# K projection by quarters, the residual added in DRAM, the first convolutions together at the end, and rotary tables scaled in place: one change to an attention and convolution kernel

## The chip, the cores and the metric

The kernel runs on one core of one Trainium2 chip. The metric is the device time of one execution in microseconds (us). All data are fp32. Engines are called by their profile names: PE (TensorE, matrix multiplication; PEld is its weight load), DVE (VectorE), ACT (ScalarE), POOL (GpSimd) and SP (SyncE, which here only issues DMAs). DMAs with addition on the way (accumulates) are issued by POOL, plain loads and stores mostly by SP.

## The reference

Two layers on x of shape (4, 1024, 32, 32): 4 batches, 1024 channels, 1024 tokens (pixels). The first is attention with rotary angles, an RMS norm of q and of k over all channels, 16 heads of 64, a projection, an RMS norm and a residual:

```python
x = hidden_states.reshape(B, C, N).transpose(0, 2, 1)
residual = x
qkv = (x @ w_qkv.T + b_qkv).reshape(B, N, 3, nh, hd)
q, k, v = (qkv[:, :, 0], qkv[:, :, 1], qkv[:, :, 2])
q = _apply_rope(q, cos, sin)
k = _apply_rope(k, cos, sin)
q = _rmsnorm(q.reshape(B, N, inner), q_norm_w).reshape(B, N, nh, hd)
k = _rmsnorm(k.reshape(B, N, inner), k_norm_w).reshape(B, N, nh, hd)
scores = jnp.einsum('bqhd,bkhd->bhqk', q, k) * scale
attn = jax.nn.softmax(scores, axis=-1)
ctx = jnp.einsum('bhqk,bkhd->bqhd', attn, v).reshape(B, N, inner)
out = ctx @ w_proj.T
out = _rmsnorm(out, norm_out_w)
out = out + residual
```

The second is a bottleneck block. Its norms are over all batches, so no later convolution can start before the first one has seen all four:

```python
out = jax.nn.relu(_bn(_conv(x, w1, b1, 1, 0), g1, be1))    # 1x1, 1024 -> 256
out = jax.nn.relu(_bn(_conv(out, w2, b2, 1, 1), g2, be2))  # 3x3, 256 -> 256
out = _bn(_conv(out, w3, b3, 1, 0), g3, be3)               # 1x1, 256 -> 1024
out = jax.nn.softplus(residual_scale)[0] * out
out = x + out
return jax.nn.relu(out)
```

## The kernel before

**Stages.** For each batch b: the projections q, k and v, attention, and the projection y of its result. Channels lie on the 128 partitions in 8 blocks, tokens along the free axis, so q(b), k(b) and y(b) are 8 blocks of 128 x 1024. After the four batches come the first convolutions conv1 of batches 1, 2 and 3, then the 3x3 convolution (with Winograd's transform) and the last 1x1 convolution. conv1(0) alone stands earlier, between q(1) and k(1) (L937 to L941). x1 = layer 0's result goes through DRAM in x1d: o_norm writes it (L805), read_back (L899) fetches it for conv1, and the end reads it again (L1194).

**Projections.** They use Strassen's scheme in Winograd's form. `project` (L283) is one level: 7 products of 512 x 512 x 512 blocks in place of 8, each in 4 groups of 4 matmuls of 128x512, 112 in all. `project2` (L415), "by quarters", applies the scheme again within each of the 7: 49 products, each 4 matmuls of 128x256, 196 in all. It costs more sums: DVE makes four inner sums of operands for each k (L446), adds products that can't be summed in PSUM (L466, L468), and makes block sums of 128x1024 (L487); ACT copies products out of PSUM (L501 to L544). Its weights come as 7 loads of 256 KB for each of the 7 outer products (L421): three straight from the weights or the one-level sums, four from wd2 in DRAM, which `prepare` (L393) has written before (4 loads, 4 DVE sums, 4 stores of 256 KB). One load is issued by SP as one of the wring's 8 slots comes free. q, v and y of b = 1 to 3 go by quarters; k of every batch, and all of b = 0, go by one level. wd2 has three planes: WQ, WV, WP. WQ's seven and three of WV's are prepared in attention of b = 0, the other four of WV in y(0), WP's in attention of b = 1.

**Rotary angles and norm.** `qk_proj` (L552) sums the squares over the channels beside the projection; the q, k bias goes into the Square pass (L560) and, for q, into the rotation. `inverse_rms` (L651) makes the sums over partitions on PE (ss_q, ss_k, ss_y), a reciprocal on DVE, and spreads it over all partitions through DRAM (inv_d, L670 and L671). `rope` (L676) multiplies cos and sin tables by it (L680 to L682; cosT x norm goes to a buffer of its own, rc, sinT x norm into total), and then rotates the 8 blocks one by one ("turn": two DVE operations of 128x1024, then two accumulating DMAs of 256 KB on POOL, L694).

**Attention** (L728). 16 steps (8 pairs of heads for each half of the tokens), each 14.6 us of PE: scores, Exp on ACT, the denominators' sums on DVE, and the product with v. The list `extra` (L773) puts one step of other work, such as a `prepare`, behind each.

**Residual.** o_norm (L798) runs beside the next batch's q stage: for each block DVE scales y (L803), POOL accumulates x from DRAM onto y in SBUF (y<-in_x_dram, L804, 512 KB), and when this has landed it writes y to x1d (x1df<-y, L805, 512 KB). The last batch uses last_norm, with DVE adding x.

**What sets the order.** PE's order is that of the source. The order on the other engines is made by a scheduler, so that a line may be issued earlier than where it stands. Within the source, a small pacing machine places the side work: `after(n, step)` (L243) runs a step n products later, `waiting` is a queue of (cost, step) of which `product_done` (L246) takes as many as DVE has room for, and `rest` (L262) drains both, for instance at the end of v (L947).

**Buffers.** y(b) and k(b) share one buffer (pool kp), so k(b+1) can be written only when y(b) has been stored. x(b+1), attention's probabilities and x1 read back share another (xp). The 16 "units" of scratch for q by quarters lie in a room that later holds v.

Of the kernel before, what the change touches and what calls it, by code (L numbers as in the profile page):

```python
# [11 lines left out]
F32 = mybir.dt.float32  # L12
AF = mybir.ActivationFunctionType
# [72 lines left out]
def program(ctx, tc, x, wblk, w2, w3, vecs, cos, sin, out, bad):  # L86
# [24 lines left out]
    def col(name, i=0):  # L111
        return vec[:, COL[name] + i : COL[name] + i + 1]
# [31 lines left out]

    wd = dram.tile([4 * NG, len(SUMS), P, NH * P], F32, name=f"wd{u}")

    wd2 = dram.tile([3, len(OUTER), len(SUMS), P, CH], F32, name=f"wd2{u}")
    dens = dram.tile([P, CH], F32, name=f"dens{u}")
    inv_d = dram.tile([3 * B, N], F32, name=f"inv_d{u}")
    norms_done = list(range(3 * B))  # L150
# [2 lines left out]
    with tc.tile_pool(name=f"st{u}", bufs=2) as st, ExitStack() as s:  # L153
# [10 lines left out]

        cosT = tp.tile([P, N], F32, tag="cos", name="cosT")
        sinT = tp.tile([P, N], F32, tag="sin", name="sinT")
        ident = None
        if bad is None:
            ident = kv.tile([P, P], F32, name="ident")
# [38 lines left out]
        def flat(t):  # L208
            return t.rearrange("p a b -> p (a b)")
# [37 lines left out]
        def after(n, step):  # L247
            later.append((pace["at"] + n, step))
# [13 lines left out]
            spend(cost)  # L262
            step()

        def rest():
            while later or waiting:
                product_done()

        def sums(ts, bs, i):
# [279 lines left out]
                    product_done(H2)  # L549
            pace["hold"] = False  # L550

        def qk_proj(b, base, bs, ts, bias, dst, tag, w1=None, two=None):  # L552

            total = acc.tile([P, N], F32, tag="tot", name=f"sq{tag}_{b}")
            seen = set()

            def outs(g):
                return [dst[:, f, h] for f in (g, g + NG) for h in half]

            def squares(at, c, bias=None):  # L560
                bias = 0.0 if bias is None else bias
                if c not in seen:
                    seen.add(c)
                    nc.scalar.activation(total[:, half[c]], at, AF.Square, bias=bias)
                    return
                sq = temp(f"sq_{tag}_{b}")
                nc.scalar.activation(sq, at, AF.Square, bias=bias)  # L567

                def more():
                    spend(TT)  # L570
                    nc.vector.tensor_tensor(total[:, half[c]], total[:, half[c]], sq, ALU.add)  # L571

                after(0.5, more)

            if two is None:
                project(b, base, bs, ts, outs, bias, squares, False, tag, w1)
                return total

            def ready(c):
                ob, tb = (int(i) - 1 for i in c)  # L580
                for i in range(NG):
                    f = ob * NG + i
                    after(
                        0.5 * (i // 2 + 1),
                        lambda f=f: squares(dst[:, f, half[tb]], tb, col(bias, f) if bias else None),
                    )

            project2(b, two[0], base, two[1], two[2], two[3], dst, False, tag, ready)
            return total
# [83 lines left out]

            after(4, root)

        def rope(b, dst, total, eps, scale, w, tag, rc, biased=True):  # L676

            def tables():  # L680
                nc.vector.tensor_tensor(rc, cosT, total, ALU.mult)
                nc.vector.tensor_tensor(total, sinT, total, ALU.mult)  # L682

            def turn(f):
                k, other = dst[:, f, :], big_temp(f"{tag}s_{b}_{f}")
                for i, (t, table) in enumerate(((other, total), (k, rc))):
                    if w is not None:
                        nc.vector.scalar_tensor_tensor(t, k, w[i][:, f : f + 1], table, ALU.mult, ALU.mult)  # L688
                    elif biased:
                        nc.vector.tensor_tensor(t, k, table, ALU.mult)  # L690
                    else:
                        nc.vector.scalar_tensor_tensor(t, k, col("bq", f), table, ALU.add, ALU.mult)
                for i in range(2):
                    nc.gpsimd.dma_start(dst[i::2, f, :], other[1 - i :: 2, :], accum_op=ALU.add)  # L694

            def then():
                waiting.append((4 * TT, tables))
                for f in range(NT):
                    waiting.append((4 * TT, lambda f=f: turn(f)))

            inverse_rms(total, eps, scale, f"{tag}_{b}", then)
# [26 lines left out]
        def attention(b, c, q_all, k_all, v, probs_, late, ready, extra):  # L728
# [4 lines left out]
            for hp in range(NHP):  # L733
# [35 lines left out]
                if hp % 2 == 1:  # L769
                    for r in ready:  # L770
                        mean_of_v(q_all, *r)
                    ready.clear()
                if extra:  # L773
                    extra.pop(0)()
                if hp % 2 == 0:
                    continue
# [21 lines left out]
        def o_norm(b, total, ys):  # L798


            def norm(f):
                y = ys[:, f, :]
                nc.vector.scalar_tensor_tensor(y, y, col("ow", f), total, ALU.mult, ALU.mult)  # L803
                nc.gpsimd.dma_start(y, x[b, f * P : (f + 1) * P, :], accum_op=ALU.add)  # L804
                nc.gpsimd.dma_start(x1d[f, :, b * N : (b + 1) * N], y)  # L805
# [20 lines left out]
        def conv1_weights(name):  # L826
            return [[block(W1, f, ih, f"c1_{name}_{f}_{ih}") for ih in range(2)] for f in range(NPT)]
# [75 lines left out]
        def x_tile(b):  # L903
            return xp.tile([P, NT, N], F32, tag="x", name=f"x_{b}")
# [19 lines left out]
        nc.sync.dma_start(cosT, cos)  # L924
        for i in range(2):

            nc.sync.dma_start(sinT[i::2, :], sin[1 - i :: 2, :])
        queue_sums(ts[0], xs[0])
        room = v_room("rq_0")
        for b in range(B):  # L930
# [4 lines left out]
            tq = qk_proj(b, WQ, xs[b], ts[b], "bq", q_all, "q", w1 if b == 0 else None, two)  # L935
            rope(b, q_all, tq, eps_q, HD / C, None, "q", flat(room[:, 2:3, :]), b == 0)
# [48 lines left out]
            if b + 1 < B:  # L985
                xs[b + 1] = x_tile(b + 1)
                ts[b + 1] = t_tiles(b + 1)
                rows = (0, 1, 4, 5, 2, 3, 6, 7)
                for j in range(NT):

                    def load(b=b, i=rows[j]):
                        for c in range(NCH):
                            load_x(b + 1, c, (i,))

                    after(3 + 1.5 * j, load)
                for i in range(0, NH, 2):

                    def queue(b=b, i=i):
                        waiting.append((7 * TT, lambda: sums(ts[b + 1], xs[b + 1], i)))

                    after(3 + 1.5 * (2 * i + 3) + 2, queue)
                if b == 0:
                    for k in range(3, len(OUTER)):
                        after(5 * (k - 3) + 0.5, lambda k=k: after(4, prepare(1, WV, k, big_pieces)))
            else:
                back = {B - 3: x_tile(b + 1)}
                for i in range(NT):
                    after(8 + 1.5 * i, lambda i=i: read_back(B - 3, (i,)))
            yt[b] = kp.tile([P, NT, N], F32, tag="k", name=f"y_{b}")
            two = (2, *in_place(q_all, tc_, yt[b], False)) if b > 0 else None  # L1010
            ty = qk_proj(b, WP, q_all, tc_, None, yt[b], "y", None, two)
# [3 lines left out]
                xr = v_room("xr")  # L1015
                last_norm(b, ty, yt[b], xr)

        back[B - 2] = kv.tile([P, NT, N], F32, tag="q", name="back")
        read_back(B - 2)
# [342 lines left out]
```

## Time and profile before

| what | value |
|---|---|
| time, median of 3 runs | 2771.21 us (2770.35 to 2775.1) |
| the profiled execution | 2769.1 us |
| its span | 2767.3 us |
| mean granted PE clock | 0.995 |
| DMA moved in the span | 390.27 MB, mean 141 GB/s |

Some of its groups of instructions (line, engine, operation, out<-in, shapes and count; then busy us, mean ns of one; then idle time before them and what ended it):

```profile
L756 DVE TENSOR_TENSOR den<-den,p 128x1024 f32<-128x1024 f32 x384 | 470.5, 1225 | 41.4 <-ACT p L752 0.9
L571 DVE TENSOR_TENSOR sqk<-sqk,sq_k 128x512 f32<-128x512 f32 x56 | 37.9, 688 | 56.1 <-ACT sq_k L567 54.8
L316 ACT COPY k<-pa_k 128x512 f32<-128x512 f32 x48 | 28.1, 586 | 116.3 <-PE pa_k L297 116.3
```

A DVE operation on 128x512 takes 0.688 us, on 128x1024 about 1.22. Each fp32 matmul shows as two PE records, and PEld's weight loads overlap them. Three more stages, in the columns of a table by stage (window, length, busy us of each engine with its count, mean granted clock, DMA share, GB/s):

```profile
361.00:448.00 87.00, 87.00 (x408) 31.70 (x408) 82.25 (x76) 47.86 (x54) 25.40 (x31) 1.00 0.52 164
536.16:632.49 96.33, 96.33 (x226) 42.76 (x226) 59.98 (x74) 18.58 (x32) 22.75 (x35) 1.00 0.72 243
2443.10:2526.40 83.30, 83.30 (x203) 36.66 (x202) 45.26 (x70) 14.12 (x21) 3.23 (x4) 1.00 0.65 232
```

They are three pairs of attention steps of b = 0 with their preparations, y(0), and conv1 of batches 1, 2 and 3.

### The profile page before, as it was taken

What the parts mean: (1) busy time and instruction counts of PE and PEld (TensorE: products, weight loads), DVE (VectorE), ACT (ScalarE), POOL (GpSimd) and SP (SyncE); (2) the same over time, 40 slices, a digit from 0 to 9 for tenths busy, and PEclk for the clock granted to TensorE, in tenths of its full rate; (3) what the DMA queues carried; (4) which work ended last, traced back from release to release, by engine and by line L of the source; (5) the groups of instructions that cost most, each with busy time, mean ns of one, the idle gap of its engine ahead of it and who ended that gap; (6) DMA issues with size and microseconds to landing.
All of it is one profiled execution on the core that took longest, in us unless ns stands there. A gap on an engine that the chain in (4) does not pass through costs nothing.

```text
span 2767.3 us, 31322 instructions
## 1 busy us (share of the span) xinstructions
PE 2727.7 (99%) x11242; PEld 1561.1 (56%) x11242; DVE 1955.9 (71%) x2213; ACT 1029.5 (37%) x1407; POOL 368.9 (13%) x419
## 2 busy tenths in 40 slices
PE   9999999999999999999999999999999999999997
PEld 4449533347647633488648433688467333856853
DVE  4355599765645898787648777887648977767987
ACT  1221455422222455423222555332223555222266
POOL 1033022121010121101011100101201110100000
PEclk9999999999999999999999999999999999999999
DMA  5366254276555552167567210459647010672165
GB/s 206 107 171 174 82 168 139 73 268 195 177 137 152 149 156 79 41 206 210 177 143 196 53 24 16 149 151 264 148 131 201 16 24 16 202 270 84 62 216 211
DMA packets 213157, 390.27 MB, mean 141 GB/s; under 512 B 24768, under 2 KB 97008, under 8 KB 212992
## 3 DMA queue, kind: packets, MB, share of 16 engines
q1 hardware_dynamic: 181856, 284.24, 32.7%
q0 software_dynamic: 31136, 103.92, 15.0%
q8 instruction: 92, 1.51, 0.2%
q14 instruction: 73, 0.60, 0.1%
HBM read 260.88 MB, written 76.86 MB: 122 GB/s over the span
## 4 chain that ended last, share of the span: by engine, by line
PE 97%; DMA 2%; DVE 1%; ACT 0%; issue 0%; SPq 0%; ACTq 0%
PE sc L745 16%; PE cx L762 16%; PE p_v L436 9%; PE p_y L441 9%; PE p_q L441 9%; PE pa_k L297 8%; PE c L833 4%; PE pc_k L297 4%; PE c L1266 4%; PE pa_q L297 2%; PE pa_v L305 2%; PE pb_k L297 2%; PE pa_y L297 2%; PE c2x L1127 2%; PE c2y L1127 2%; DMA w_q<-wdf 1%
## 5 line engine op out<-in xcount | busy, mean ns | idle before, releaser
L756 DVE TENSOR_TENSOR den<-den,p 128x1024 f32<-128x1024 f32 x384 | 470.5, 1225 | 41.4 <-ACT p L752 0.9
L752 ACT ACTIVATE p<-sc 128x1024 f32<-128x1024 f32 x512 | 476.2, 1043 | 55.0 <-PE sc L745 53.5
L745 PE MATMUL sc<-q,k 64*128 64x512 f32 x2048 | 457.2, 596 | 2.2 <-DVE v L468 1.6
L762 PE MATMUL cx<-p,v 128*64 128x512 f32 x2048 | 453.6, 595 | 0.0
L745 PEld LDWEIGHTS sc<-q,k 64*128 64x128 f32 x2048 | 190.9, 186 | 266.3 <-issue 121.4
L762 PEld LDWEIGHTS cx<-p,v 128*64 128x64 f32 x2048 | 141.4, 137 | 304.3 <-issue 304.3
L726 POOL TENSOR_SCALAR q<-q,vec 128x512 f32<-128x512 f32 x64 | 125.9, 1973 | 665.8 <-DVE q L725 665.8
L767 ACT COPY q<-cx 128x512 f32<-128x512 f32 x64 | 37.5, 586 | 357.2 <-PE cx L762 357.2
L441 PE MATMUL p_y<-q,w_y 128*128 128x256 f32 x696 | 157.5, 380 | 0.0
L436 PE MATMUL p_v<-w_v,x 128*128 128x256 f32 x696 | 157.1, 379 | 0.0
L441 PE MATMUL p_q<-to,w_q 128*128 128x256 f32 x672 | 154.5, 384 | 0.0
L754 DVE TENSOR_TENSOR den<-p 128x1024 f32<-128x1024 f32 x64 | 76.5, 1196 | 99.8 <-ACT p L752 99.8
L441 PEld LDWEIGHTS p_y<-q,w_y 128*128 128x128 f32 x696 | 131.8, 190 | 20.7 <-issue 2.5
L436 PEld LDWEIGHTS p_v<-w_v,x 128*128 128x128 f32 x696 | 132.2, 190 | 19.3 <-issue 1.4
L441 PEld LDWEIGHTS p_q<-to,w_q 128*128 128x128 f32 x672 | 129.2, 193 | 19.6 <-issue 1.6
L787 DVE RECIPROCAL rec<-dn 128x512 f32<-128x512 f32 x32 | 107.3, 3353 | 28.8 <-PE dn L781 28.7
L1266 PE MATMUL c<-h,w 128*128 128x512 f32 x256 | 110.3, 592 | 0.9 <-ACT h L1170 0.9
L1266 PEld LDWEIGHTS c<-h,w 128*128 128x128 f32 x256 | 48.6, 190 | 62.1 <-issue 54.3
L694 POOL DMA_DIRECT2D k<-ks x64 | 55.3, 1010 | 205.0 <-DVE k L688 123.9
L571 DVE TENSOR_TENSOR sqk<-sqk,sq_k 128x512 f32<-128x512 f32 x56 | 37.9, 688 | 56.1 <-ACT sq_k L567 54.8
L316 ACT COPY k<-pa_k 128x512 f32<-128x512 f32 x48 | 28.1, 586 | 116.3 <-PE pa_k L297 116.3
L571 DVE TENSOR_TENSOR sqq<-sqq,sq_q 128x512 f32<-128x512 f32 x56 | 38.4, 690 | 44.5 <-ACT sq_q L567 42.0
(535 smaller groups left out, 4116.8 us busy)
## 6 DMA issues: line engine op xcount, KB each, us to landing
w_q<-wd2f SPq DMA_DIRECT2D x84, 256.0 KB
w_v<-wd2f SPq DMA_DIRECT2D x84, 256.0 KB
w_y<-wd2f SPq DMA_DIRECT2D x84, 256.0 KB
wd2f<-w_pre POOLq DMA_DIRECT2D x68, 256.0 KB, 2.7
x<-in_x_dram SPq DMA_DIRECT2D x64, 256.0 KB
q<-qs POOLq DMA_DIRECT2D x64, 256.0 KB, 5.1
k<-ks POOLq DMA_DIRECT2D x64, 256.0 KB, 5.2
inv<-rec SPq DMA_DIRECT2D x256, 64.0 KB
```

Of the source, the lines that this page charges most:

```text
L297: nc.tensor.matmul(o, w[:, i, :], r(i), start=first and i == 0, stop=last and i == NH - 1, skip_group_check=True,)
L436: nc.tensor.matmul(o[:, q].rearrange("p (g f) -> p g f", g=2), r[:, i, q * P : (q + 1) * P], wt[:, :, i, :], skip_group_check=True, **at,)
L441: nc.tensor.matmul(o[:, q], wt[:, q, i, :], r[:, i, :], skip_group_check=True, **at)
L726: nc.gpsimd.tensor_scalar(cx, cx, col("bv", hp), None, ALU.add)
L745: nc.tensor.matmul(sc[:, j], k_all[d, hp, t * P : (t + 1) * P], q_all[d, hp, at], start=True, stop=bad is not None,)
L752: nc.scalar.activation(p, sc, AF.Exp)
L756: nc.vector.tensor_tensor(d_, d_, p, ALU.add)
L762: nc.tensor.matmul(o[j * HD : (j + 1) * HD, :], v[:, t, h0 : h0 + HD], probs[t][:, j], start=(t == 0), stop=(t == N // P - 1),)
L787: nc.vector.reciprocal(r, dn)
L833: nc.tensor.matmul(o, w[f][ih][:, ii, :], ys[:, i, half[c]], start=(i == 0), stop=(i == NT - 1))
L1127: nc.tensor.matmul(o[:, r * TR * TC : (r + 1) * TR * TC], uw[2 * h + r, j][:, i * PL + f * P : i * PL + (f + 1) * P], vt[b, i][:, 2 * h + ...
L1266: nc.tensor.matmul(os[i], w3t[k][f // NH][:, f % NH, :], h2[b, k][:, half[c]], start=(k == 0), stop=(k == NPT - 1),)
```

## The change

- k of b = 1 to 3 goes by quarters. wd2 gets a fourth plane for WK. WV's seven are all prepared in attention of b = 0, with WK's first; WK's other six in y(0). In k the bias is added by an ACT pass of its own, in place, before the square; q keeps the old way (`bias_later`).
- o_norm no longer adds x: it writes y to x1d. In the source of the next batch, before its attention, stand 8 accumulates from x in DRAM onto x1d in DRAM.
- conv1(0) leaves its place between q(1) and k(1) and comes after conv1(2) at the end; its x1 is read back into xp's buffer.
- cosT and sinT are multiplied by the norm in place; rc is gone. After the last turn of every rope but the last, both are loaded again (three SP DMAs, 1 MB).
- For b > 0 `rest` leaves four of the waiting steps, which are turns of k, for attention, where they come ahead of `extra`.

```diff
-    wd2 = dram.tile([3, len(OUTER), len(SUMS), P, CH], F32, name=f"wd2{u}")
+    wd2 = dram.tile([4, len(OUTER), len(SUMS), P, CH], F32, name=f"wd2{u}")
...
+        def load_tables():
+            nc.sync.dma_start(cosT, cos)
+            for i in range(2):
+
+                nc.sync.dma_start(sinT[i::2, :], sin[1 - i :: 2, :])
+
...
-        def rest():
-            while later or waiting:
+        def rest(leave=0):
+            while later or len(waiting) > leave:
                 product_done()
...
                 for i in range(NG):
                     f = ob * NG + i
-                    after(
-                        0.5 * (i // 2 + 1),
-                        lambda f=f: squares(dst[:, f, half[tb]], tb, col(bias, f) if bias else None),
-                    )
+
+                    def done(f=f):
+                        at = dst[:, f, half[tb]]
+                        if bias and not bias_later:
+                            nc.scalar.activation(at, at, AF.Identity, bias=col(bias, f))
+                        squares(at, tb, col(bias, f) if bias and bias_later else None)
+
+                    after(0.5 * (i // 2 + 1), done)
...
             def tables():
-                nc.vector.tensor_tensor(rc, cosT, total, ALU.mult)
-                nc.vector.tensor_tensor(total, sinT, total, ALU.mult)
+                for t in (sinT, cosT):
+                    nc.vector.tensor_tensor(t, t, total, ALU.mult)
...
-                for i, (t, table) in enumerate(((other, total), (k, rc))):
+                for i, (t, table) in enumerate(((other, sinT), (k, cosT))):
...
+                if f == NT - 1 and (b, tag) != (B - 1, "k"):
+                    load_tables()
...
-                if extra:
+                if waiting:
+                    next_waiting()
+                elif extra:
                     extra.pop(0)()
...
                 nc.vector.scalar_tensor_tensor(y, y, col("ow", f), total, ALU.mult, ALU.mult)
-                nc.gpsimd.dma_start(y, x[b, f * P : (f + 1) * P, :], accum_op=ALU.add)
                 nc.gpsimd.dma_start(x1d[f, :, b * N : (b + 1) * N], y)
...
-            if b == 1:
-                w = conv1_weights(b)
-                for c in range(NCH):
-                    for f in range(NPT):
-                        conv1(b - 1, f, c, w, yt[b - 1])
             k_all = kp.tile([P, NT, N], F32, tag="k", name=f"k_{b}")
-            tk = qk_proj(b, WK, xs[b], ts[b], "bk", k_all, "k")
-            rk = acc.tile([P, N], F32, tag="tot", name=f"rk_{b}")
-            rope(b, k_all, tk, eps_rms, 1.0 / C, (wqk_other, wqk), "k", rk)
+            two = (3, *beside(xs[b], ts[b], units)) if b > 0 else None
+            tk = qk_proj(b, WK, xs[b], ts[b], "bk", k_all, "k", None, two)
+            rope(b, k_all, tk, eps_rms, 1.0 / C, (wqk_other, wqk), "k")
...
-            rest()
+
+            rest(leave=4 if b > 0 else 0)
...
-            if b < 2:
-                which, base = ((0, WQ), (2, WP))[b]
-                todo = [(which, base, k) for k in range(len(OUTER))]
             if b == 0:
-                todo += [(1, WV, k) for k in range(3)]
+                todo = [(which, base, k) for which, base in ((0, WQ), (1, WV)) for k in range(len(OUTER))]
+                todo.append((3, WK, 0))
+            elif b == 1:
+                todo = [(2, WP, k) for k in range(len(OUTER))]
...
+            if b > 0:
+                for f in range(NT):
+                    nc.gpsimd.dma_start(
+                        x1d[f, :, (b - 1) * N : b * N], x[b - 1, f * P : (f + 1) * P, :], accum_op=ALU.add
+                    )
...
                 if b == 0:
-                    for k in range(3, len(OUTER)):
-                        after(5 * (k - 3) + 0.5, lambda k=k: after(4, prepare(1, WV, k, big_pieces)))
+                    for k in range(1, len(OUTER)):
+                        after(4 * k - 3.5, lambda k=k: after(3, prepare(3, WK, k, big_pieces)))
...
-        for b in (B - 3, B - 2):
+        for b in (1, 2, 0):
+            if b == 0:
+                back[0] = x_tile("back")
+                read_back(0)
             for c in range(NCH):
                 for f in range(NPT):
                     conv1(b, f, c, w, back[b])
```

More of the change, by code (lines that the diff above doesn't have):

```diff
@@ L550, in project2, with qk_proj @@
             pace["hold"] = False
-        def qk_proj(b, base, bs, ts, bias, dst, tag, w1=None, two=None):
+        def qk_proj(b, base, bs, ts, bias, dst, tag, w1=None, two=None, bias_later=False):
             total = acc.tile([P, N], F32, tag="tot", name=f"sq{tag}_{b}")
@@ L674, in inverse_rms, with rope @@
             after(4, root)
-        def rope(b, dst, total, eps, scale, w, tag, rc, biased=True):
+        def rope(b, dst, total, eps, scale, w, tag, biased=True):
             def tables():
-                nc.vector.tensor_tensor(rc, cosT, total, ALU.mult)
-                nc.vector.tensor_tensor(total, sinT, total, ALU.mult)
+                for t in (sinT, cosT):
+                    nc.vector.tensor_tensor(t, t, total, ALU.mult)
             def turn(f):
                 k, other = dst[:, f, :], big_temp(f"{tag}s_{b}_{f}")
-                for i, (t, table) in enumerate(((other, total), (k, rc))):
+                for i, (t, table) in enumerate(((other, sinT), (k, cosT))):
                     if w is not None:
@@ L923, in program @@
         load_x(0, 1)
-        nc.sync.dma_start(cosT, cos)
-        for i in range(2):
-            nc.sync.dma_start(sinT[i::2, :], sin[1 - i :: 2, :])
+        load_tables()
         queue_sums(ts[0], xs[0])
@@ L934, in program @@
             two = (0, *beside(xs[b], ts[b], units)) if b > 0 else None
-            tq = qk_proj(b, WQ, xs[b], ts[b], "bq", q_all, "q", w1 if b == 0 else None, two)
-            rope(b, q_all, tq, eps_q, HD / C, None, "q", flat(room[:, 2:3, :]), b == 0)
-            if b == 1:
-                w = conv1_weights(b)
-                for c in range(NCH):
-                    for f in range(NPT):
-                        conv1(b - 1, f, c, w, yt[b - 1])
+            tq = qk_proj(b, WQ, xs[b], ts[b], "bq", q_all, "q", w1 if b == 0 else None, two, True)
+            rope(b, q_all, tq, eps_q, HD / C, None, "q", b == 0)
             k_all = kp.tile([P, NT, N], F32, tag="k", name=f"k_{b}")
-            tk = qk_proj(b, WK, xs[b], ts[b], "bk", k_all, "k")
-            rk = acc.tile([P, N], F32, tag="tot", name=f"rk_{b}")
-            rope(b, k_all, tk, eps_rms, 1.0 / C, (wqk_other, wqk), "k", rk)
+            two = (3, *beside(xs[b], ts[b], units)) if b > 0 else None
+            tk = qk_proj(b, WK, xs[b], ts[b], "bk", k_all, "k", None, two)
+            rope(b, k_all, tk, eps_rms, 1.0 / C, (wqk_other, wqk), "k")
             v = v_proj(b, xs[b], ts[b], (lambda v, b=b: in_place(xs[b], ts[b], v, True)) if b > 0 else None)
-            rest()
+            rest(leave=4 if b > 0 else 0)
             psum_for("att")
             todo = []
-            if b < 2:
-                which, base = ((0, WQ), (2, WP))[b]
-                todo = [(which, base, k) for k in range(len(OUTER))]
             if b == 0:
-                todo += [(1, WV, k) for k in range(3)]
+                todo = [(which, base, k) for which, base in ((0, WQ), (1, WV)) for k in range(len(OUTER))]
+                todo.append((3, WK, 0))
+            elif b == 1:
+                todo = [(2, WP, k) for k in range(len(OUTER))]
             made = []
@@ L1002, in program @@
                 if b == 0:
-                    for k in range(3, len(OUTER)):
-                        after(5 * (k - 3) + 0.5, lambda k=k: after(4, prepare(1, WV, k, big_pieces)))
+                    for k in range(1, len(OUTER)):
+                        after(4 * k - 3.5, lambda k=k: after(3, prepare(3, WK, k, big_pieces)))
             else:
-                back = {B - 3: x_tile(b + 1)}
+                back = {1: x_tile(b + 1)}
                 for i in range(NT):
-                    after(8 + 1.5 * i, lambda i=i: read_back(B - 3, (i,)))
+                    after(8 + 1.5 * i, lambda i=i: read_back(1, (i,)))
             yt[b] = kp.tile([P, NT, N], F32, tag="k", name=f"y_{b}")
@@ L1016, in program @@
                 last_norm(b, ty, yt[b], xr)
-        back[B - 2] = kv.tile([P, NT, N], F32, tag="q", name="back")
-        read_back(B - 2)
+        back[2] = kv.tile([P, NT, N], F32, tag="q", name="back")
+        read_back(2)
         w = conv1_weights("last")
```

## The prediction

> **What bounds the kernel now.** I read five views in this order: the busy table, the chain of work that ended last, the busy time by stage, the waits, and the chain inside one q stage. First the page:
>
> ```profile
> PE 2727.7 (99%) x11242; PEld 1561.1 (56%) x11242; DVE 1955.9 (71%) x2213; ACT 1029.5 (37%) x1407; POOL 368.9 (13%) x419
> ...
> PE 97%; DMA 2%; DVE 1%; ACT 0%; issue 0%; SPq 0%; ACTq 0%
> ```
>
> TensorE is busy for all but 39.6 us of the 2767.3 us span and makes 97% of the chain. So a change pays for two things: PE time taken away, and PE idle time made or removed. Everything else is cover, until it is used up. By stage (columns: window, length, busy time of each engine with its count, granted clock, DMA share, GB/s):
>
> ```profile
> 632.49:725.40 92.91, 88.92 (x402) 76.56 (x401) 65.51 (x86) 30.13 (x51) 12.84 (x18) 0.96 0.81 233
> 725.40:753.63 28.23, 28.23 (x73) 12.23 (x73) 8.61 (x12) 4.89 (x8) 1.13 (x2) 1.00 0.27 89
> 753.63:849.80 96.17, 96.17 (x225) 42.59 (x225) 39.08 (x42) 19.96 (x33) 13.86 (x16) 1.00 0.50 123
> 849.80:935.46 85.66, 85.58 (x402) 74.16 (x400) 65.66 (x82) 22.08 (x38) 9.81 (x12) 1.00 0.69 186
> 1168.89:1253.78 84.89, 84.89 (x394) 74.60 (x394) 74.26 (x92) 25.63 (x45) 7.77 (x4) 1.00 0.66 203
> 1253.78:1346.33 92.55, 87.36 (x401) 75.45 (x401) 68.22 (x91) 30.08 (x51) 12.74 (x18) 0.98 0.82 236
> 1346.33:1443.00 96.67, 96.67 (x232) 42.47 (x232) 44.61 (x50) 22.20 (x37) 14.93 (x18) 1.00 0.51 127
> ```
>
> The rows are q(1), conv1(0), k(1), v(1), y(1), q(2), k(2). A k stage is one Strassen level, 112 matmuls of 128x512; a q, v or y stage is two levels, 196 matmuls of 128x256. y(1) takes 84.89 us with PE never idle and DVE at 74.3: that is what a two-level stage costs when it is fed. q(2) has the same matmuls and takes 92.55. Why is in its chain and in the waits:
>
> ```profile
> 1268.16 22.66 PE p_q L441 x104
> 1290.82 0.02 issue
> 1290.83 10.80 DMA w_q<-wdf
> ...
> 1308.60 0.02 issue
> 1308.61 8.05 DMA w_q<-wdf
> ...
> PE p_q L441 <- DMA w_q<-wdf: 13.9, 4, 4.7
> POOL x1df L805 <- DMA y<-in_x_dram: 30.6, 6, 8.8
> ```
>
> Weight loads of q are late while o_norm's residual accumulates (y<-in_x_dram, 8 x 512 KB) and x1d writes (8 x 512 KB) of the batch before are under way. From 1281 to 1303 the DMA share is 0.99. A q stage is 92.91 or 92.55 long (93.0 in q(3), 1847.98 to 1940.97), less 84.89 for its matmuls and 0.57 for the ss_y sums that fall in it: stalls of 7.5, 7.1 and 7.5, 22.1 us in all.
>
> **What the Trainium skill says.** *DMA: Bandwidth & Descriptors*, section "Issuing engines are not separate DMA queues": DMAs of all issuing engines run on the same 16 DMA engines and interleave. The trace agrees: loads issued by SP are late in the stretch that POOL's transfers fill. The same page, "SWDGE vs HWDGE vs iDMA": accumulation in flight is for GpSimd's queue only; here every accumulate is POOL's. The same page, "Rules for kernel authors": an accumulate reads its destination and writes it later, so an access of the same bytes has to wait for it. Hence the new accumulate into x1d must wait for the landing of the write of the same block. No page prices a DRAM to DRAM accumulate.
>
> **The change part by part.**
>
> *k by quarters, b = 1 to 3.* Removed: 112 matmuls, each shown as two records that advance 0.429 us, 0.858 each: 96.1 us. Added: 196 matmuls of 128x256 at 2 x 0.2165 = 0.433: 84.9. That is -11.24 us a stage, -33.7 in all. On PE this lies fully on the path. What must keep up:
> - DVE. 28 inner sums, 29 adds of products and 14 sums of squares at 0.688 (71 x 0.688 = 48.8), 10 block sums of 128x1024 at 1.22 (12.2), tables 2.45, a reciprocal 1.75, four of q's turns at 2 x 1.285 (10.3): 75.5 of 85 us. The v stage: 51.4 of its own, the other turns of q (10.3) and two of k (5.1), tables 2.45, reciprocal 1.75, four squares 2.75: about 74. y(1) ran at 74.3 without a stall, so I cost the load at nothing and only its bunching below.
> - ACT. The bias is now a pass of its own in place (16 x 0.69 = 11 us): about 40 of 85 us. When two quarters are done in one product of 1.73 us, two Identity-and-Square pairs of 1.3 us stand ahead of the copy that frees PSUM. PE is two products (3.46 us) ahead, so 0 to 1 us an event, 0 to 4 a stage. I take 0.8 a stage: +2.5.
> - Weights: 196 x 64 KB = 12.8 MB in 85 us, as y has at share 0.66; nothing.
> - Preparing WK's seven planes (each 4 loads, 4 DVE sums of 3.0 us in all, 4 stores). 15 prepares now run in b = 0's attention in place of 10, so all its pairs of heads look like those of 361 to 448, where DVE is busy 82.25 of 87 us and PE never stops. In y(0) six prepares stand where four stood (DVE 60 to 66 of 96 us, DMA share 0.72 to about 0.84); SP's loads of w_y queue behind prepare loads with 6 to 8 us in hand. 0 to 3 us, I take 1.5; 0.5 more in b = 0 for table reloads ahead of w_k loads (bound 0 to 1.5).
>
> *Residual from DRAM to DRAM.* The source line stands at the start of the next batch's attention, but the instruction order of the changed kernel has, on POOL's queue, three writes of x1d, three accumulates, then write and accumulate by turns, all ahead of q's inverse norm. Nothing else on POOL separates them from the writes. So they stay in the q stage: same 8 writes, same 8 accumulates, the target in DRAM instead of SBUF. y's buffer is free earlier, which k needs only 85 us later. For a DRAM to DRAM accumulate there is no row. From the queue shares between 1278 and 1305 (54.8% for 3.67 MB on POOL's queue, 37.2% for 3.41 MB on SP's) I estimate 2.7 us of all engines for an accumulate of 512 KB and 1.2 for a plain one. Lower bound 1.2, upper bound twice 2.7. With 3.5, the stage needs 8 x 0.8 = 6.4 us more engine time; the share over the whole stage is 0.82, so the free 17 us take some, and weights being late turns part of it into stall: I take +2 a stage, +6 in all, with ends -5 and +15 a stage. What waits behind a slow accumulate on POOL is inv_df<-rms_q and with it q's tables and turns, covered by DVE's free 9 us in k.
>
> *All first convolutions at the end.* conv1(0), 28.2 us of PE with the DMA share at 0.27, leaves the place between q(1) and k(1) and comes back after conv1(2): 0 on PE. q(1)'s leftover DMA loses a quiet stretch, as b = 2 and 3 never had one. At the end 4 MB more are read into a buffer that is free only when conv1(1) ends (about 27.5 us after the start), behind waiting stores on SP's queue. conv1(0) needs its first row 55 us after the start: I estimate the last rows are issued some 50 to 55 us after it, row by row needed 0.86 us apart. In 2443 to 2526 the DMA share is 0.65 at 232 GB/s. 0 to 3 us, I take 1.5.
>
> *Tables in place.* The same two DVE operations, but cosT and sinT (1 MB) are loaded anew after every rope's last turn, seven times, by three SP DMAs which wait for that turn. In the v stages of b = 1 to 3 they stand on SP between w_v_4_0 and w_v_4_1: the weight loads behind them wait for DVE's q_7. Weights are some 6.7 to 8.5 us ahead of their use; q_7 may be later than this by 0 to 4 us. I take 1.5 a stage: +4.5. k's tables wait 1 to 3 us for the reload, inside DVE's free 10 us. After k's last turn the reload lies in attention, where DMA is at 0.11.
>
> *k's last four turns in attention.* 4 x 2.57 us of DVE in the first four heads' steps; a step is 14.6 us of PE, and DVE has 11.0 of it (176.5 of 233 us over 16 steps in attention(2)), so 13.6: hidden. Steps with such a turn get no weight preparation. It takes 10 us of DVE work out of v.
>
> Sum: -33.7 + 2.5 + 2.0 + 6 + 1.5 + 4.5 = -17.2 on 2769.1: 2751.9. The median of the runs shown is 2771.2, 2.1 above that execution, which itself is 1.8 above its span. Since later times can lie on either, I keep the profiled one and say 2752.
>
> **The rivals.**
> 1. *DRAM to DRAM accumulates saturate the DMA engines longer.* One mechanism: at 5.4 us each, 8 x 2.7 = 21.6 us more engine time a stage, against some 17 us free in q; the weights of q's middle and of k's first products come late. For: the share is 0.99 in the middle already, and weights have been late at just that point; k needs 12.8 MB instead of 7.3. Against: k(2) has half its DMA time free. Above about +7.7 us a stage (2 + 17.2/3) the change loses; with all of 12 to 13 us turning into stall it is 2769.1 - 17.2 - 6 + 38 = 2784.
> 2. *The q stage gets lighter.* The accumulates no longer hold y, writes go first, weights get their turn: the stalls fall from 7.4 to 1 or 2 us: -17 in place of +6, 2729. Against: bytes and order are the same.
> 3. *Cover of DVE and ACT runs out in k and v.* Both at 75 of 85 us in bunches, with waits for tables and accumulates between: 3 us a stage more, 6 x 3 = 18: 2770, or 4 us at a time only in k: 2764. Against: y(1) at 74.3.
> 4. *The residual does not move into attention.* Not a separate time: it is what the order shows and is in the forecast. If the accumulates did run there, q would lose most of its 22 us stall and rival 2's time holds.
>
> **How the numbers follow.** Forecast 0.55, its own range 2740 to 2765; rival 1 0.15; rival 2 (or 4) 0.15; rival 3 0.15. What a measurement tells from no change is 0.2%, 5.5 us: faster is below 2765.7. Faster: 0.53 + 0.15 + 0.06 = 0.74; same: 0.02 + 0.02 + 0.05 = 0.09; slower: 0.13 + 0.04 = 0.17. The range, from most of rival 2 to part of rivals 1 and 3: 2727 to 2777.
>
> **What would show it.** k stages of about 85 to 88 us with 196 matmuls; q stages of 90 to 100 us whose chain still has w_q behind x1df<-in_x_dram; the landing time of that transfer against 8.5 us; in v a wait of PE for w_v just after the table reload; the end without a wait for x_back of more than 3 us. I am wrong if q exceeds 100 us (rival 1), falls below 88 (rival 2), or k and v exceed 89 with waits for DVE or ACT (rival 3).

## The result: no change, and the profile after

The changed kernel takes 2771.25 us (median of 6 runs, 2765.56 to 2778.29), the kernel before 2772.09 (6 runs beside it). The ratio is 0.9998, 95% interval 0.9982 to 1.0013: no change. The profiled execution has a span of 2767.7 us against 2767.3. The page, first the busy row, then the shares of the chain that ended last:

```profile
PE 2702.5 (98%) x11746; PEld 1657.4 (60%) x11746; DVE 2095.3 (76%) x2406; ACT 1080.2 (39%) x1494; POOL 383.6 (14%) x447
...
PE 88%; DMA 5%; DVE 2%; ACT 2%; issue 1%; SPq 0%; POOL 0%; POOLq 0%; DVEq 0%; ACTq 0%
```

PE is busy 25.2 us less than before (2727.7), and idle that much more: 65.2 us for 39.6. The chain went through PE for 97% and does so now for 88%. So the gain was made, and spent on waits. Where they stand is read by stage. The table takes each stage from its first matmul to the first of the next ("everything else" is mostly the start of the 3x3 convolution, 1.6 us longer, with PE at half its clock for a while; four of the ten experiments show this too):

| stage | before, us | after, us | difference | forecast |
|---|---|---|---|---|
| k(1), k(2), k(3) | 96.1, 96.9, 96.9 | 86.8, 86.8, 86.8 | -29.5 | -31.2 |
| y(0) | 96.2 | 111.4 | +15.2 | +1.5 |
| v(1), v(2), v(3) | 85.8, 86.6, 86.6 | 88.8, 88.0, 89.6 | +7.4 | +4.5 |
| q(1), q(2), q(3) | 92.9, 92.6, 93.0 | 92.4, 95.8, 97.0 | +6.7 | +6 |
| conv1, all batches | 28.2 + 83.2 | 110.6 | -0.8 | +1.5 |
| everything else | | | +1.4 | +0.5 |
| sum | | | +0.4 | -17.2 |

The rows that answer to those shown of before are y(0), q(2), k(2), v(2) and the four conv1, in the columns of the table by stage (window, length, busy time of PE, PEld, DVE, ACT and POOL with counts, granted clock, DMA share, GB/s):

```profile
536.16:647.54 111.38, 101.15 (x225) 43.81 (x226) 66.51 (x84) 18.63 (x32) 29.80 (x48) 0.95 0.78 267
...
1233.64:1329.41 95.77, 88.23 (x401) 75.85 (x401) 68.39 (x91) 30.06 (x51) 12.27 (x18) 0.96 0.84 229
1329.41:1416.36 86.95, 86.20 (x402) 74.33 (x402) 70.53 (x92) 36.30 (x62) 8.07 (x10) 1.00 0.66 180
1416.36:1504.04 87.68, 85.97 (x401) 73.85 (x399) 71.69 (x91) 25.71 (x44) 11.50 (x14) 1.00 0.73 201
2414.38:2526.00 111.62, 111.62 (x269) 49.33 (x269) 48.33 (x75) 17.49 (x25) 3.23 (x4) 1.00 0.64 220
```

k is what the forecast said, a two-level stage with PE idle for under 1 us. The four conv1 run without any wait. The surprise is the first row: y(0) has the matmuls of before and takes 15 us longer, 10 of them idle. The other 5 are in PE's own busy time, 101.15 us for 96.33, at a mean granted clock of 0.95. The waits in y(0), first the two longest of PE and one of DVE, then the two longest of SP's queue (what was waited for, us in total, times, longest):

```profile
PE pa_y L304 <- DVE w_y_0b L238: 4.7, 1, 4.7
PE pa_y L304 <- ACT y L323: 3.4, 1, 3.4
...
DVE w_y_2b_s L236 <- DMA w_y_2b<-in_wblk_dram: 10.2, 1, 10.2
```

```profile
SPq L398 <- DMA wd2f<-pre: 37.6, 6, 9.4
SPq L221 <- DMA wd2f<-w_pre: 13.7, 3, 12.2
```

In the same view of the kernel before, SP's queue has one entry of this kind:

```profile
SPq L391 <- DMA wd2f<-pre: 13.4, 4, 5.3
```

SP's two entries are waits for buffers. `w_pre` are four of the eight slots of the weight ring, held by the fifteenth preparation (WK's first, the last one in b = 0's attention) until its stores have landed; SP stands before them for 12.2 us around the start of y(0). `pre` are the buffers of y(0)'s own preparations: the next one's loads wait until the last one's stores have landed. All of y(0)'s weight loads go through this one queue. PE's second wait, put down to ACT, leads there too: the chain goes back from ACT's copy through sums of DVE to the load of w_y_2b, for which DVE stood 10.2 us, and from this load to SP, which had waited for a store of `pre`. The timeline of SP shows it, after and then before (start us, us, what was issued):

```profile
545.93 6.44 SPq L810 DMA_DIRECT2D inv<-rec  x8
552.41 2.15 SPq L398 DMA_DIRECT2D pre<-in_wblk_dram  x4
...
557.48 3.19 SPq L221 DMA_DIRECT2D w_y_0b<-in_wblk_dram  x4
```

```profile
540.20 4.98 SPq L795 DMA_DIRECT2D inv<-rec  x8
545.22 3.20 SPq L391 DMA_DIRECT2D pre<-wdf  x6
548.47 2.04 SPq L214 DMA_DIRECT2D w_y_0b<-in_wblk_dram  x4
```

Both stages begin at 536.2. The loads of w_y_0b are issued 9 us later than before. PE wants their sums at 563.7 in both kernels, and gets them at 568.4 in the changed one.

### The profile page after: what moved, and what is told of

Same layout as the page of the kernel before. It is cut to its first block, busy times and chain, and to the rows that moved or that the text cites. A ratio compares the mean times of both kernels' runs of the same rounds, so it can differ in the third digit from the quotient of the medians.

```text
span 2767.7 us, 32938 instructions
## 1 busy us (share of the span) xinstructions
PE 2702.5 (98%) x11746; PEld 1657.4 (60%) x11746; DVE 2095.3 (76%) x2406; ACT 1080.2 (39%) x1494; POOL 383.6 (14%) x447
## 4 chain that ended last, share of the span: by engine, by line
PE 88%; DMA 5%; DVE 2%; ACT 2%; issue 1%; SPq 0%; POOL 0%; POOLq 0%; DVEq 0%; ACTq 0%
PE sc L758 16%; PE cx L775 16%; PE p_y L448 9%; PE p_v L443 8%; PE p_q L448 8%; PE p_k L448 7%; PE c L847 4%; PE c L1281 4%; PE pa_v L312 2%; PE pa_q L304 2%; DMA w_q<-wdf 2%; PE pa_k L304 2%; PE c2x L1142 2%; PE c2y L1142 2%; PE dn L796 1%
## 5 line engine op out<-in xcount | busy, mean ns | idle before, releaser
L448 PE MATMUL p_k<-to,w_k 128*128 128x256 f32 x672 | 153.1, 381 | 2.3 <-ACT k L538 1.5
L448 PEld LDWEIGHTS p_k<-to,w_k 128*128 128x128 f32 x672 | 126.7, 190 | 23.5 <-ACT to L538 2.8
L705 POOL DMA_DIRECT2D q<-qs x64 | 55.7, 1020 | 289.5 <-issue 170.7
```

The source lines that it names most:

```text
L448: nc.tensor.matmul(o[:, q], wt[:, q, i, :], r[:, i, :], skip_group_check=True, **at)
```

## The experiments

Ten kernels ran; the time of the kernel before beside them was 2770.43 to 2772.31 us (medians). Unless a ratio is given, each is one profiled execution, compared with the span 2767.7 by stages. How far a stage moves by itself is seen in the kernels whose edit does not touch it: y(0) took 108.7 to 113.7 us in the changed kernel and four others, the three q stages together 281.1 to 288.5 in the changed kernel and six others, and the three v stages 265.6 to 269.1 in the changed kernel and seven others.

**1. WK's six preparations out of y(0)** into v(0); the fifteenth stays in attention.

```diff
+            if b == 0:
+                for k in range(1, len(OUTER)):
+                    after(4 * k - 3.5, lambda k=k: after(2, prepare(3, WK, k, big_pieces)))
             v = v_proj(...)
...
-                if b == 0:
-                    for k in range(1, len(OUTER)):
-                        after(4 * k - 3.5, lambda k=k: after(3, prepare(3, WK, k, big_pieces)))
```

> WK's six preparations move from y(0) into v(0); the one in the last step of b = 0's attention stays. Span of the changed kernel 2767.7 us, its y(0) 111.4 us against 96.3 before. Theory A (the weights of y(0) are late because of queues and buffers: first because the 15th preparation holds four slots of the weight ring until 8 us into y(0), then because SP stands before preparation loads that wait for stores): the first stall stays and the later ones go, y(0) about 105, span about 2761. Theory B (16 DMA engines are simply full with six preparations more): y(0) about 96, span about 2753. v(0) has DMA share 0.55 and DVE free for 56 of 102 us: 101.7 to 104 either way.

Measured: 2786.39 us, span 2784.6. y(0) is 96.5 us, as in Theory B, but v(0) went from 101.7 to 135.6. v(0) and y(0) by stage, then waits in v(0):

```profile
201.74:337.32 135.58, 106.13 (x905) 105.02 (x903) 60.91 (x74) 14.58 (x26) 36.76 (x58) 0.89 0.68 202
570.65:667.11 96.46, 96.46 (x228) 42.58 (x225) 50.86 (x61) 18.53 (x32) 17.06 (x24) 1.00 0.52 177
```

```profile
DVE ks L699 <- DMA k<-ks: 31.3, 5, 9.3
PE pa_v L312 <- DVE w_v_2b L238: 18.7, 1, 18.7
```

Six preparations in v(0) share three big buffers with k's eight turns. A turn waits until an older turn's accumulate (k<-ks) has landed, DVE, which takes its work in the source's order, stands there for 31.3 us in all, and PE behind it. My sentence that v(0) had room, since DMA and DVE were half free, was wrong: buffers had none. For y(0), Theory A fails as it was put (about 105, the first wait staying). SP still stands 12.1 us before `w_pre`, but without preparation loads behind it nothing is late: the fifteenth preparation alone costs nothing. Theory B's number came out, but this does not show that the DMA engines were the limit, since the edit took the six preparations out of SP's queue as well as their bytes off the engines (share 0.52).

**2. All seven of WK's in v(0).** As 1, with `range(len(OUTER))` there, each 3.5 products after the last in place of 4, and without `todo.append((3, WK, 0))` in attention.

> All seven of WK's preparations in v(0), so the last of attention's (b = 0) is a step earlier and y(0) has none. Theory A: y(0) falls another 9 us against the run with six in v(0), to about 96, span about 2752. Theory B: no difference in y(0) between six and seven in v(0) beyond 2 us.

Measured: 2794.4 us, span 2792.6; y(0) 96.2, v(0) 136.7. No difference between six and seven in y(0), because 1 had already removed the whole of its loss. So the two causes do not simply add: the fifteenth preparation is paid for only while the six stand in y(0).

**3. The fifteenth preparation alone** moved to the start of v(0); six stay in y(0).

```diff
+            if b == 0:
+                after(0.5, lambda: after(2, prepare(3, WK, 0, big_pieces)))
             v = v_proj(...)
...
-                todo.append((3, WK, 0))
```

> Of the changed kernel only WK's first preparation moves, from the last step but one of b = 0's attention to the start of v(0); six stay in y(0). Theory A1 (the first stall of y(0), 4.7 us of waiting and 6.8 us at half clock, comes from the fifteenth preparation: its four buffers hold the weight ring, and SP's whole list of y(0) starts 5 us later): the first stall goes, y(0) from 111.4 to about 101 to 103. Theory B1 (six preparations in y(0) are too many for SP's list whatever comes before): y(0) stays above 108. v(0) 101.7 to 104.

Measured: 2763.21 us, span 2761.4; v(0) 101.7, y(0) 103.2. The first wait is gone. Of PE's waits in y(0) the longer one that is left, then y(0)'s row:

```profile
PE pa_y L304 <- ACT y L323: 2.9, 1, 2.9
...
536.09:639.30 103.21, 99.84 (x228) 43.60 (x225) 64.95 (x82) 18.68 (x32) 27.15 (x43) 0.97 0.79 267
```

Theory A1 holds: 8.2 of the 15.2 us go with one preparation, give or take the 2 to 3 us by which y(0) moves by itself. Full DMA engines were not what made the first wait: from 550 to 568 they are full in this run and in the kernel before (share 1.00 and 1.01), where PE never waits; in the changed kernel, where PE stands, they have room (0.83), since SP's list came later. The other 7.0 belong to six preparations in place of four.

**4. Sums one product after the loads,** in y(0): `after(3, prepare(...))` becomes `after(1, prepare(...))`.

> In y(0) the sums of each of WK's six preparations follow their loads by one product in place of three, so that the buffers' stores land before the next preparation's loads are due; same bytes, same order otherwise. Theory A (SP stands before a load whose buffer waits for a store, 37.6 us in y(0), and w_y's loads stand behind it): the later stalls shrink, y(0) 111.4 to 100 to 106. Theory B (the DMA engines are full): y(0) stays at 109 to 113. Theory C: DVE, which takes its work in order, now waits for the preparation's loads, and y(0) gets longer than 113.

Measured: 2768.53 us, span 2766.7; y(0) 111.2. SP's wait for `pre` fell from 37.6 to 23.2 us and the later waits of PE went, but the first grew to 12.8. The chain shows that the preparation's stores, now earlier, stand on POOL before attention's last means (the additions of v's bias), on which y(0)'s own operands wait. Inconclusive: it moved the cost between two queues. How the 7 us that experiment 3 leaves divide between SP's queue and the DMA engines (share 0.78) isn't separated by any run. It also corrects a sentence at the head of this document: in these stages only SP's and POOL's orders are the scheduler's; the kernel asks for the source's order on DVE and ACT (`manual_schedule`, L928 of the changed one), as it does on PE.

**5. Tables reloaded by POOL:** `nc.sync` becomes `nc.gpsimd` in `load_tables`, but for the first load.

> The reloads of cosT and sinT are issued by POOL in place of SP, all else as changed. Theory (SP's queue: the reloads wait for DVE's last turn of q, and the w_v loads behind them wait with them): the waits for w_v go, v of b = 1 to 3 falls from 88.5, 87.7 and 89.6 to about 86, span down 6 to 8 us to about 2760. Rival (the extra megabyte, or DVE and ACT running late at the start of v, makes v longer): v stays at 87.5 to 89.5, span within 2 us.

Measured: 2771.02 us, span 2769.2; v 89.3, 89.5 and 91.3. The theory falls as put: over the three v stages PE's wait for w_v falls from 3.4 to 1.1 us, but 4.1 us of waiting for a sum of DVE (L458) come in its place, and v is no shorter. DVE's waits in v(1):

```profile
DVE sinT L693 <- DMA sinT<-in_sin_dram: 6.1, 1, 6.1
```

The reload takes its time after q's last turn whoever issues it. From SP, the loads behind it are late; from POOL, DVE arrives at k's tables first and stands 6.1 us before them, with v's own sums behind.

**6. The accumulates in attention.** Each is queued behind an instruction of POOL that belongs to the next attention.

```diff
+        residual = []
         def mean_of_v(q_all, c, hp, w):
...
-            nc.gpsimd.tensor_scalar(cx, cx, col("bv", hp), None, ALU.add)
+            done = nc.gpsimd.tensor_scalar(cx, cx, col("bv", hp), None, ALU.add)
+            if residual:
+                with tc.issue_after(done.ins):
+                    nc.gpsimd.dma_start(*residual.pop(0), accum_op=ALU.add)
...
             if b > 0:
                 for f in range(NT):
-                    nc.gpsimd.dma_start(
-                        x1d[f, :, (b - 1) * N : b * N], x[b - 1, f * P : (f + 1) * P, :], accum_op=ALU.add
-                    )
+                    residual.append((
+                        x1d[f, :, (b - 1) * N : b * N], x[b - 1, f * P : (f + 1) * P, :]
+                    ))
```

> Each accumulate of x onto x1d is queued on POOL behind a mean_of_v of the next attention, so that the q stage keeps the eight writes of x1d alone. Theory (the accumulates take the DMA engines from q's weights): q of b = 1 to 3 falls from 92.4, 95.8 and 97.0 to 86 to 88, span down 20 to 26 us to about 2745. Rival (the writes and q's own loads saturate the engines by themselves): q stays above 91, span down less than 8 us.

Measured: 2742.93 us, span 2741.1. q is 85.6, 85.4 and 85.4: no wait at all. q(2)'s row and chain:

```profile
1228.86:1314.23 85.37, 85.37 (x401) 74.56 (x400) 68.23 (x91) 30.09 (x51) 5.44 (x10) 1.00 0.67 207
```

```profile
1243.41 70.99 PE p_q L448 x328
```

The same chain in the changed kernel:

```profile
1248.02 22.66 PE p_q L448 x104
...
1270.70 11.79 DMA w_q<-wdf
...
1291.85 9.90 DMA w_q<-wdf
```

The theory holds, beyond its number: 28.8 us off q (285.2 to 256.4). Both the kernel before and the changed one paid for eight accumulates in the q stage; in attention they land in 7.1 us at the median, and attention stays at 233.3 (the last at 234.0).

**7. The residual as before,** the rest as changed: o_norm gets its accumulate onto y back, and the eight in DRAM go.

> The residual alone goes back to the way of before (x accumulated onto y in SBUF, then y written to x1d), all else as changed. Theory (an accumulate in DRAM costs the engines some 0.6 us more than one in SBUF, 41.4% of 95.8 us against 37.7% of 92.55 for POOL's queue): q of b = 1 to 3, 92.4, 95.8 and 97.0, falls to 92.5 to 94, 4 to 6 us in all, span about 2763. Rival (the 6.7 us more in q come from what stands around it, conv1(0)'s place or the preparations): q stays at 95 in sum of three 285 or more.

Measured: 2762.81 us, span 2761.0; q 92.3, 94.7 and 91.8, 278.8 in sum against 285.2. The theory holds in direction: 278.8 lies with the kernel before (278.4) and below all seven kernels that accumulate in DRAM in the q stage (281.1 to 288.5). By this pair, eight accumulates in DRAM cost q 2.1 us a stage more than eight in SBUF; with that spread the cost may be anything from about 1 to 3 us. In q(2) of the changed kernel an accumulate landed in 9.3 us at the median, and a write of x1d in 8.7 (before: 8.5 and 6.0).

**8. k's bias left out** (b = 1 to 3): the Identity pass is removed.

> The addition of k's bias in b = 1 to 3 is left out (16 ACT passes a stage less); all else as changed. Theory (ACT's backlog at a finished quarter holds PE): k from 86.8 to 85.6, and v loses the 0.9 us at its start, 6 us in all, span about 2762. Rival (the 1.1 us in k are DVE's tables and turns): k stays at 86.5 to 87.

Measured: 2758.85 us, span 2757.1; k 85.4 in each, v 87.4, 88.4 and 88.0. k's row:

```profile
740.72:826.10 85.38, 85.38 (x402) 74.56 (x401) 71.04 (x93) 28.32 (x50) 8.17 (x10) 1.00 0.67 183
```

ACT's 8 us less give 1.4 us a stage: PE then never waits in k. The theory holds. The bias pass costs k 4.3 us and v some 2.6 in sum (of the 10.6 us of span; the rest is mostly q and y(0), which this edit doesn't touch); DVE at 71 of 85 us costs k nothing.

**9. Preparations spread, accumulates in attention.** On top of 6:

```diff
+            if b == 0:
+                for k in range(2):
+                    after(3 * k + 0.5, lambda k=k: after(2, prepare(0, WQ, k, big_pieces)))
             tk = qk_proj(...)
...
+            if b == 0:
+                for k in range(2, 4):
+                    after(3 * k - 5.5, lambda k=k: after(2, prepare(0, WQ, k, big_pieces)))
             v = v_proj(...)
...
-                todo = [(which, base, k) for which, base in ((0, WQ), (1, WV)) for k in range(len(OUTER))]
-                todo.append((3, WK, 0))
+                todo = [(which, base, k) for which, base in ((0, WQ), (1, WV)) for k in range(len(OUTER))][4:]
+                todo += [(3, WK, k) for k in range(4)]
...
-                    for k in range(1, len(OUTER)):
-                        after(4 * k - 3.5, lambda k=k: after(3, prepare(3, WK, k, big_pieces)))
+                    for k in range(4, len(OUTER)):
+                        after(5 * (k - 4) + 0.5, lambda k=k: after(4, prepare(3, WK, k, big_pieces)))
```

> The accumulates stand in attention (as in resid_attn, 2741.1 us span), and the 21 preparations are spread: two of WQ in the first seven products of k(0), two in those of v(0), before the rotation's turns need the same three buffers; fourteen in attention; three of WK in y(0), spaced and lagged as the four of before. Theory A (buffers and queues, not the engines): k(0), v(0) and attention stay at 96.9, 101.7 and 233.3, y(0) falls from 113.7 to 96 to 98, span about 2724, ratio to before about 0.985. Theory B (the work of 21 preparations has no free place): what leaves y(0) comes back in k(0) and v(0), span 2735 or more.

Measured: 2728.13 us, ratio to before 0.9849 (0.9832 to 0.9865), span 2725.9. v(0) stays at 101.7; k(0) and y(0):

```profile
103.55:201.32 97.77, 97.17 (x233) 42.55 (x232) 56.27 (x69) 23.61 (x38) 28.37 (x42) 1.00 0.73 210
...
536.30:632.54 96.24, 96.24 (x229) 42.67 (x225) 57.37 (x70) 18.56 (x32) 20.65 (x31) 1.00 0.65 221
```

Theory A holds. Each of the 21 preparations has a place, at a cost of 0.9 us in all (k(0) at 97.8 for 96.9), if they come while the buffers are free. y(0) has three of them here, one fewer than in the kernel before.

**10. Tables from POOL, and k's tables four steps later,** on top of 9; `rest(leave=6)`, and `product_done` takes no waiting step after q's last turn until `pace["at"]` has gone on by 4.

> On spread (span 2725.9, v of b = 1 to 3 at 89.5, 89.6 and 88.5): the tables are reloaded from POOL's queue, so that w_v's loads have no wait ahead of them on SP, and DVE, which takes its work in order, comes to k's tables four steps later, when the reload has landed; six turns of k go to attention. Theory (v pays a wait at either end of the reload: w_v behind it on SP, or DVE before it): v falls to 86 to 87 in each, span about 2717, ratio to before about 0.981. Rival (v's loss is DVE's and ACT's load alone): v stays above 88, span within 2 us of 2726.

Measured: 2725.45 us, ratio to before 0.9837 (0.982 to 0.9853), span 2721.6; v 87.3, 87.3 and 87.4. PE's waits that are left in v, over all three batches:

```profile
PE sc L765 <- DVE v L475: 2.3, 3, 0.8
PE p_v L443 <- ACT k L594: 2.2, 3, 0.7
```

The theory holds in direction: both waits for the reload are gone, 5.6 us off v. What stays is ACT's backlog of k at the start of v and the passage to attention, 2 us a stage, so v stopped at 87.3 and not at 86. Attention gave 1.5 us back. By their intervals 9 and 10 are not told apart; both are faster than the kernel before and the changed one.

## Why the prediction was wrong

It said 2752 us, faster with a chance of 0.74; 2771.25 lies inside its range, and no change was given 0.09. Its own steps:

- *k by quarters*: right, -29.5 in the k stages (-30.3 with conv1, which carried q's sums before) against -31.2. ACT's lag was put at 0.8 a stage in k and is 1.4 (experiment 8), though the bias passes are shorter than reckoned: 8 us of ACT a stage, not 11. The load of DVE was rightly costed at nothing.
- *Preparing WK's planes*: the step that failed. "0 to 3 us, I take 1.5" for y(0) measured 15.2, and the text had two reasons for its number that do not hold. "6 to 8 us in hand" was reckoned for y(0)'s list alone; the fifteenth preparation, costed inside attention ("all its pairs of heads look like those of 361 to 448"), holds half of the weight ring 8 us into y(0) and puts SP's list back by some 6 us, so that w_y_0b's loads, behind y(0)'s own preparation loads, are issued 9 us later. That is 8.2 us (experiment 3), the six for four another 7.0, whose split between SP's queue and the DMA engines stays open. And no wait was priced with what follows it, PE at half clock. I looked at DVE's and the DMA engines' share, which had room, and not at who holds which buffer until when.
- *Residual*: right in place, and in size within the spread of q. Its accumulates stayed in q, +6.7 for +6; experiment 7 gives them 6.4. That it comes within 1 us of the forecast is luck, as q moves by 7 us from kernel to kernel. POOL's accumulates waited 43.2 us in all for the landing of the writes in q(2), as the prediction had inferred. Rival 2, with the accumulates still in q, did not occur. What rival 4 added is real: with the accumulates in attention q lost 28.8 us, where the prediction's sum for this case is 23 (+6 to -17).
- *Tables in place*: the mechanism right, +7.4 in v for +4.5. Behind SP's reload PE waited for w_v in v(1) to v(3), 3.4 us in sum; some 2.6 are the bias pass's backlog (experiment 8), which the text had put into k alone.
- *First convolutions*: right. conv1 takes 110.6 us and no row of x_back was late; the 1.5 us kept for it were not needed.
- By span the forecast missed by 17.6 us: 13.7 in y(0), 2.9 in v, 1.7 in k, 0.7 in q, -2.3 in conv1 and 0.9 elsewhere. None of the rivals named y(0). Rival 3 had the right sum by luck, since it put the loss into k and v; rival 1 did not occur.

## What to carry to other kernels

When a stage gets more side work, list for each buffer ring who holds its slots at the stage's start and until which landing: a DMA queue that stands before a held slot delays every load behind it, whatever room the share of the engines shows. One such delay may cost nothing, as in experiment 1; a second one on the same queue then finds no slack left. Moving a DMA in the source does not move it in time if a scheduler may issue it as soon as it is ready; tie it to an instruction of the stage where it is to run. Price a wait of the matrix engine of some 4 us at one and a half times its length: here 4.7 and 3.4 us of waiting cost 7.3 and 4.9.

## What was unexpected of the hardware

After a wait PE ran at half its clock. The record of the granted clock has two such stretches in y(0), 6.8 us from 566.6 and 3.4 us from 617.8, and the matmuls after the first wait show it. First the row of 564 to 572, then the group of eight matmuls (minimum, median and maximum in ns, first and last start):

```profile
564.00:572.00 8.00, 3.59 (x5) 1.55 (x6) 4.02 (x7) 1.86 (x3) 2.45 (x5) 0.66 0.95 338
```

```profile
L304 PE MATMUL pa_y<-to,w_y_0b x8: 592/1061/1192, 568.4 to 574.0; 128*128 128x512 f32 x8
```

1192 ns in place of 592. PE was at work for some 8 us of the two stretches, and these explain about 4 of the 5 us by which its busy time grew. The Trainium skill, "TensorE: Matmul & The Clock Gate", section "Part 1: The HAM clock gate (the "warmup" mystery)", says that the clock halves after an idle window of about 3.4 us and comes back after a busy one of that length. The lengths here, 3.4 and 6.8 us, agree, and in each of the twelve traces the stretches start whole multiples of 3.41 us apart. The wait that is needed was shorter than the page says, and depends on where it falls: from k(0) to the last convolution, in all twelve traces, each of the 35 waits of PE of 3.4 us and more was followed by such a stretch, none of the 35 between 1 and 2 us, and 14 of the 27 in between. One wait of 2.4 us at the start of the 3x3 convolution is the same in all twelve kernels and was followed by it in five; the 1.6 us of the table's "everything else" are this. The changed kernel has three more stretches in its q stages, as the kernel before has; experiments 9 and 10 have none before the 3x3 convolution.
